# Four graph layers in one kernel: seams of layer 0, and group ends and maxima of layers 1 to 3

## Chip, cores and metric

One core of a Trainium2 chip runs the whole kernel in one launch. The metric is the time of one execution in device microseconds (us). TensorE (PE) does the matrix products, PEld is its weight load, VectorE (DVE), ScalarE (ACT) and GpSimd (POOL) do the rest; SyncE (SP) issues most DMAs, POOL some of them.

## What is computed

There are N = 2708 nodes with F = 512 features and one 0/1 adjacency matrix `adj` with about 1.2% ones and a full diagonal, all in float32. Four layers follow each other, and after each `x = layernorm(x + layer(x, adj))`. Cut to what matters:

```python
# layer 0: H = 4 heads of 128; _batchnorm over all nodes; att is the same for both uses
Xw  = einsum('hnd,hde->hne', Xh, W)
sig = sigmoid(f1[:, :, None] + f2[:, None, :])
att = masked_softmax(adj * sig, adj != 0)
Xn  = batchnorm(att @ Xw)                       # first pass over the attention
emb = batchnorm(elu(Xn @ Wm.T + bm) + Xn)       # encoder block
Y   = elu((att @ emb) @ W.T)                    # second pass
out = batchnorm(elu(Y @ Wd.T + bd) + Y)         # decoder block
# layer 1
x1 = (A @ (x @ W + b)) / deg[:, None]
# layer 2
e = (x @ edge_w) @ (x @ edge_w).T               # symmetric
x2 = adj * softmax(x @ node_w, 0) * softmax(where(adj > 0, e, NEG), 1) @ (x @ weight) + bias
# layer 3
x3 = softmax((x @ Wq + bq) @ (x @ Wk + bk).T / sqrt(F) + 2 * adj) @ (x @ Wv + bv)
```

## The kernel before

N is 21 blocks of 128 rows and a last one of 20 (REST; Q = 32). The code is written in the order of the work, and a planner fixes each engine's order when the program is built, from program order and its own estimate of when operands are ready; `tc.issue_after` puts instructions behind a given one on their engine. Engines then run strictly in that order.

**Layer 0** keeps everything transposed: attention weights are made tile by tile, 128 sources by half of the targets (1354) by two heads. `attention_pass` runs twice. In each, four rounds (half `hf`, head pair `p`) go over the 22 blocks in `ORDER`, the REST block in place 11. `form` makes a tile `t` (four buffers): tanh on ACT (L385, two operations), a masked product on DVE (L393, 2.97 us), Exp on ACT (L394). Then twelve matrix instructions add it to `po` (L460; each float32 `matmul` call is two of them). In the first pass, `p == 0` also prepares the mask `a` (L374, L375) and stores it to `adj_d`. Column sums come from a product with ones (`psm`, L483), in places 4 to 19 of `p == 1` for two tiles at once, added first on DVE (L477). Some tiles are stored to DRAM (`kept`, L442) and loaded in the second pass by SP (L445), where the other tiles load `a` from `adj_d` (L358) and `count` finds zeros (L335).

`keep` ends a round of the first pass: copies from PSUM, sums to DRAM and back as reciprocals (L583, L588, L589), and after the second round a `small_product` (vector times matrix and turned, L535, L538, L540) for the encoder's bias. After the pass, `batch_scale` gives scale1 and mean1; four products (L685) make `mqk = Wq Wk^T / sqrt(F)` for layer 3; the encoder's weights are scaled in place (L673, L677); the encoder (L713) follows with another `small_product` inside for mean1, with the second pass's first tiles formed beside it. `decode` ends a round of the second pass; its last call does the decoder's remaining products (L848) and `centre`. Then scale3 and shift3 (L521, L529), L972 on ACT, L979 on DVE, and transposes and products into `hid_hi`/`hid_lo` (L985, L117).

**Layer 1** takes four blocks of targets at a time: `raw` loads, L1037 turns them into 0/1, L1044 multiplies. Row normalizations are put off in `later`.

**Layers 2 and 3** share `softmax_layer`, with targets in 7 groups of three blocks (the last has four). `one_score` computes a tile of scores (L1203, or transposes of stored ones, L1195) and a running maximum (L1251); the REST block is split over four column sections and added up with `quarters` (L1227, L1236, L1237). `spread_max` at a group's end turns the maxima (L1263), reduces them (L1266), and spreads them over all partitions (L1269, L1274, L1287). `one_sum` subtracts, exponentiates, adds to `acc` (L1294, L1295, L1298, L1305), in layer 2 multiplies with `adj` (L1500), and multiplies with the values (L1310). It runs `lag = NT + 3` steps behind. `end` closes a group (L1360, L1370; layer 2: L1505, L1506; layer 3: L1356, then L1388, L1587).

Of the kernel before, what the change touches and what calls it, by code (L numbers as in the profile page):

```python
# [17 lines left out]
P = 128  # L18
# [11 lines left out]
def gnn_stack_kernel(  # L30
# [49 lines left out]

    def rows_tile(name):
        return big.tile([P, NT, F], F32, tag="rows", name=name)
# [71 lines left out]
    mqk_d = dram.tile([C, P, C, P], F32, name="mqk_d")  # L154
    qscale = float(1.0 / F**0.5)
# [4 lines left out]
    with ExitStack() as l0:  # L160
# [160 lines left out]
        def attention_pass(values, first, att, psum, finish, f1b=None, blocks=(), spread=None, rest=None, taken={}):  # L321
# [83 lines left out]
            for hf, (h0, w) in enumerate(HSPAN):  # L405
                for p in range(H // HP):
# [13 lines left out]
                    before = None  # L420
                    for place, jt in enumerate(ORDER):
# [8 lines left out]
                        if kept is None or first:  # L430
                            rows = n if n == P else HR
                            with ExitStack() as order:

                                for ins in taken.values() if place == 2 else ():
                                    order.enter_context(tc.issue_after(ins.ins))
                                step = form(hf, p, jt, att, prepare, f1b, t[:rows, :, :w])
                            if rest is not None:
                                rest(step)
                                rest = None
                                sums = sum_tiles()  # L440
                            if kept is not None:
                                nc.gpsimd.dma_start(kept[:n, :, :w], tv)  # L442
                        else:
                            for r in range(0, P if n == P else HB * Q, P if n == P else Q):
                                nc.sync.dma_start(t[r : r + n, :, :w], kept[:n, :, :w])  # L445
                            if p == 0 and jt in KEPT[1]:
                                count(hf, jt, att)
                        if po is None:


                            both = [
                                psum.tile([P, HP, BANK], F32, tag=f"po{q}", name="po", bufs=1)
                                for q in range(HB)
                            ]
                            po = [both[q][:, k, :] for k in range(HP) for q in range(HB)]
                        for k in range(HP):
                            h = HP * p + k
                            for q, (q0, qw) in enumerate(HCH[hf]):
                                r = 0 if n == P else q * Q
                                nc.tensor.matmul(  # L460
                                    po[HB * k + q][:, :qw],
                                    values[r : r + n, jt, h * P : (h + 1) * P],
                                    t[r : r + n, k, q0 : q0 + qw],
                                    start=(place == 0),
                                    stop=(place == NT - 1),
                                )
# [3 lines left out]
                        if prepare or not ALONE <= place < NT - LAST:  # L470
                            whole, m = t, n
                        elif place % 2 == 0:
                            before = t
                            continue
                        else:
                            whole, m = before, P
                            nc.vector.tensor_tensor(  # L477
                                whole[:n, :, :w], whole[:n, :, :w], tv, ALU.add
                            )
                        for k in range(HP):  # L480
                            for r, (q0, qw) in enumerate(SCH[hf]):

                                nc.tensor.matmul(  # L483
                                    sums[k][32 * r : 32 * r + 32, :SW],
                                    ones32[:m],
                                    whole[:m, k, q0 + qw - SW : q0 + qw],
                                    start=(place == 0),
                                    stop=(place == NT - 1),
                                )
# [62 lines left out]
        with (  # L552
# [8 lines left out]
            def keep(hf, p, po, sums):  # L561
# [10 lines left out]
                if hf == 0 and p == 1:  # L572
                    row = att.tile([P, HW], F32, tag="z", name="row", bufs=1)[:1, :F]
                    ps = small_product(po[0], mlp_w[0], prm_sb[:, B_ENC, :], row)
                    nc.vector.tensor_tensor(bias[:, 0, :], ps, prm_sb[:, MB_ENC, :], ALU.add)
# [55 lines left out]
            scale1, mean1 = batch_scale(stats, G_ENC, "bn1")  # L631

# [30 lines left out]
        with (  # L663
# [3 lines left out]

            (enc_w,) = mlp_w  # L670
            for c in range(C):
# [9 lines left out]
            mqk = emb[:, NT - 3 * C : NT - 2 * C, :]  # L681
            for c in range(C):
                ps = psum.tile([P, F], F32, tag="misc", name="ps_m", bufs=2)
                for o in range(C):
                    nc.tensor.matmul(  # L685
                        ps,
                        wqT[:, o, c * P : (c + 1) * P],
                        wkT[:, o, :],
                        start=(o == 0),
                        stop=(o == C - 1),  # L690
                    )
                nc.scalar.activation(mqk[:, c, :], ps, AF.Copy, scale=qscale)
            for o in range(C):
                nc.gpsimd.dma_start(mqk_d[o], mqk[:, :, o * P : (o + 1) * P])

            row = emb[:1, NT - 3 * C - 2 : NT - 3 * C, :]
# [8 lines left out]
            for ci, (c0, w) in enumerate(CHUNKS):  # L705
                pss = []
                for o in range(C):
# [13 lines left out]
                    if ci == 0 and o == 0:  # L721
                        pm = small_product(
                            psum.tile([P, F], F32, tag="misc", name="ps_mean", bufs=2),
                            enc_w,
                            mean1,
                            row[:, 1, :],
                        )
                        nc.vector.tensor_tensor(bias[:, 0, :], bias[:, 0, :], pm, ALU.subtract)
                        nc.vector.tensor_scalar(
                            bias[:, 1, :], bias[:, 0, :], 1.0, None, ALU.subtract  # L730
                        )
# [27 lines left out]
            spare = []  # L759

# [35 lines left out]
            def decode(hf, p, po, rb):  # L796
# [45 lines left out]
                def mlp(q, o, st, wide):  # L842
# [4 lines left out]
                    for c in range(C):  # L847
                        nc.tensor.matmul(  # L848
# [73 lines left out]
                for q in range(HB):  # L922
# [10 lines left out]
                    mlp(q, 3, st, True)  # L933

# [11 lines left out]
    with (  # L946
# [66 lines left out]
        for g in range(0, NT, G):  # L1013
# [12 lines left out]
            for jt, (j0, m) in enumerate(BLOCKS):  # L1026
# [5 lines left out]
                if m < P or w < len(group) * P:  # L1032
                    nc.vector.memset(raw[:, : len(group) * P], 0.0)
                for r in range(0, P if m == P else 2 * Q, P if m == P else Q):
                    nc.sync.dma_start(raw[r : r + m, :w], adjT[j0 : j0 + m, c0 : c0 + w])
                with tc.issue_after(ready[0].ins) if g == 0 and jt < 5 else nullcontext():
                    nc.vector.tensor_scalar(  # L1037
                        a[:, : len(group) * P], raw[:, : len(group) * P], 0.0, None, ALU.not_equal
                    )
                halves = (hid_hi, hid_lo) if m == P else (hid_hi,)  # L1040
                for it in group:
                    at = a[:, (it - g) * P : (it - g + 1) * P]
                    for k, half in enumerate(halves):
                        nc.tensor.matmul(  # L1044
                            pos[it],
# [12 lines left out]
        for y, n in later:  # L1058
            layer_norm(y, y, n)
# [13 lines left out]

    quarters = featp.tile([P, C, Q], F32, name="quarters")
    for c in range(C):
        nc.vector.tensor_tensor(
            quarters[:, c, :], ident[:, :Q], ident[:, Q : 2 * Q], ALU.add
        )
        for k in range(2, C):
            nc.vector.tensor_tensor(  # L1080
                quarters[:, c, :], quarters[:, c, :], ident[:, k * Q : (k + 1) * Q], ALU.add
            )
    quarters = quarters.rearrange("p c q -> p (c q)")
# [32 lines left out]
    def softmax_layer(  # L1116
# [12 lines left out]
        def key_order(gi):  # L1129

            late = list(range(NFULL // 2)) + [NT - 1] + list(range(NFULL // 2, NFULL))
            if not mirror:

                return late if gi else list(range(NT))
# [118 lines left out]
        def spread_max(st):  # L1253
# [3 lines left out]
            k = len(GROUPS[gi])  # L1257
            tp = psum.tile([P, C, P], F32, tag="tp", name="tp_mx")
            nm = small.tile([P, GB], F32, tag="nm", name="nm")
            dg = att.tile([P, GB, P], F32, tag="dg", name="dg", bufs=1)  # L1260
            for b, it in enumerate(GROUPS[gi]):
# [3 lines left out]
                )  # L1265
                nc.vector.tensor_reduce(  # L1266
                    nm[:n, b : b + 1], tp[:n, b, :], AX.X, ALU.max, negate=True
                )
                nc.vector.tensor_scalar(  # L1269
                    dg[:n, b, :n], ident[:n, :n], nm[:n, b : b + 1], None, ALU.mult  # L1270
                )
            pb = psum.tile([P, BANK], F32, tag="tp", name="pb")
            full = sum(BLOCKS[it][1] == P for it in GROUPS[gi])
# [15 lines left out]
        def one_sum(st, k):  # L1289
# [6 lines left out]
            if k == 0:  # L1296
                st["acc"] = att.tile([P, GW], F32, tag="acc", name="acc", bufs=1)
                nc.vector.tensor_copy(st["acc"][:, :w], e)  # L1298
                st["po"] = [
                    psum.tile([P, F], F32, tag=f"po{(GROUP * gi + b) % C}", name="po", bufs=1)  # L1300
                    for b in range(C if after is not None else len(GROUPS[gi]))
                ]
# [3 lines left out]
            if weigh:  # L1306
                weigh(e, load_a(gi, jt)[:, :w])

# [39 lines left out]
        def end(st):  # L1348
# [19 lines left out]
            for b, it in enumerate(GROUPS[gi]):  # L1368
# [15 lines left out]

                def project(b=b, it=it, n=n):
# [14 lines left out]

        def score_step(t):
# [4 lines left out]
            if k == NT - 1:  # L1406
                spread_max(states[gi])

        def sum_step(t):
            gi, k = divmod(t, NT)  # L1410
            if t == 0:
                last_values()
            one_sum(states[gi], k)
# [12 lines left out]
    with (  # L1426
# [3 lines left out]
        for gi, group in enumerate(GROUPS):  # L1430
            c0, w = GSPAN[gi]
# [273 lines left out]
```

## Time and profile before

| | |
|---|---|
| median of 3 runs | 3321.99 us (3317.25 to 3322.62) |
| profiled execution | 3319.34 us, span 3317.5 us |
| mean granted TensorE clock | 0.99 |
| layer 0, first pass / encoder / second pass with decoder | about 0 to 585 / 585 to 700 / 692 to 1197 us |
| layer 1 | about 1200 to 1511 us |
| layer 2 / layer 3 | about 1511 to 2316 / 2317 to 3317 us |
| DMA | 381 MB, mean 115 GB/s |

A profile's group is one line, engine, operation and tile: count, busy time, mean of one in ns, and after the second bar the idle time of the engine just before them with what ended it. A window gives for a stretch its length and each engine's busy time, then the granted clock (1 is full), the share of DMA time and GB/s. Times are from the span's start.

### The profile page before, as it was taken

Reading aid. Unit: us, or ns where it says so; the run is one execution under the profiler, and the core shown is the slowest. Engines: PE = TensorE matmul, PEld = TensorE weight load, DVE = VectorE, ACT = ScalarE, POOL = GpSimd, SP = SyncE. Lnnn points to the kernel's source line nnn. Section 1 sums busy time; section 2 is a strip of 40 time slices with the busy share of each in tenths; the row PEclk is TensorE's granted clock in tenths of the full one; section 3 lists DMA queues with packets and bytes.
Section 4 is the critical chain, followed back from the end, with each engine's and each line's share of the span. In section 5 each row is a group of like instructions: output and inputs, shape, how many; then the busy total and the mean of one; then the engine's idle time right before and its main releaser. Section 6 shows DMA issues by size and latency. Waiting matters only on the chain.

```text
span 3317.5 us, 30401 instructions
## 1 busy us (share of the span) xinstructions
PE 3232.7 (97%) x10920; PEld 1725.2 (52%) x10920; DVE 1971.7 (59%) x3221; ACT 1319.5 (40%) x1497; POOL 130.1 (4%) x211
## 2 busy tenths in 40 slices
PE   8998999999999999999999999999999999999999
PEld 5443444454444446885554555444455555555554
DVE  7877977767687685445135667776353443543533
ACT  6887887457868652001133333332021010110111
POOL 1100100000000000000010000000000000000000
PEclk9999999999999999999999999999999999999999
DMA  8855863335555412540044444553211111111100
GB/s 289 299 189 169 310 214 123 105 108 199 177 176 175 161 40 84 144 123 15 1 127 128 119 124 134 148 148 108 69 46 34 42 34 42 40 32 45 36 24 20
DMA packets 172550, 381.45 MB, mean 115 GB/s; under 512 B 20938, under 2 KB 115094, under 8 KB 167982
## 3 DMA queue, kind: packets, MB, share of 16 engines
q1 hardware_dynamic: 156926, 308.16, 30.7%
q0 software_dynamic: 15472, 71.33, 5.8%
q8 instruction: 86, 1.41, 0.2%
q14 instruction: 66, 0.54, 0.1%
HBM read 307.22 MB, written 71.67 MB: 114 GB/s over the span
## 4 chain that ended last, share of the span: by engine, by line
PE 76%; DVE 9%; issue 8%; DMA 4%; ACT 3%; POOL 0%; SPq 0%; DVEq 0%; POOLq 0%; ACTq 0%
PE po L1310 22%; PE ps_s L1203 17%; PE po L460 11%; PE ps_nb L1044 6%; PE ps_wide L1105 4%; DVE t L393 3%; PE ps_hid L117 2%; PE ps_sup L1447 2%; PE ps_o L1388 2%; PE ps_mlp L713 2%; PE ps_dec L848 2%; DMA a<-adj_d 1%; ACT t L394 1%; DMA a_cols<-in_adjT_dram 1%; PE psm L483 1%
## 5 line engine op out<-in xcount | busy, mean ns | idle before, releaser
L393 DVE SCALAR_TENSOR_TENSOR t<-t,a 128x2708 f32<-128x2708 f32 (+1 forms) x156 | 462.1, 2974 | 125.0 <-ACT t L385 121.1
L385 ACT ACTIVATE t<-f1b,f2h 128x1354 f32<-128x1354 f32 (+1 forms) x312 | 428.1, 1413 | 61.7 <-PE po L460 28.0
L460 PE MATMUL po<-t,xw 128*128 128x452 f32 (+3 forms) x1056 | 415.1, 557 | 15.7 <-ACT t L394 15.7
L394 ACT ACTIVATE t<-t 128x2708 f32<-128x2708 f32 (+1 forms) x156 | 382.5, 2454 | 110.5 <-DVE t L393 110.3
L1310 PE MATMUL po<-sup,e 128*128 128x512 f32 x882 | 412.4, 602 | 6.2 <-DVE e L1500 5.9
L460 PE MATMUL po<-t,emb 128*128 128x452 f32 (+3 forms) x1056 | 400.3, 547 | 12.4 <-ACT t L394 9.1
L1310 PE MATMUL po<-e,xs 128*128 128x384 f32 (+1 forms) x1176 | 407.5, 489 | 0.0
L1203 PE MATMUL ps_s<-sup,hT 128*128 128x384 f32 (+1 forms) x1176 | 406.9, 490 | 0.0
L1581 DVE SCALAR_TENSOR_TENSOR e<-a_cols,ps_s 128x384 f32<-128x384 f32 (+1 forms) x154 | 85.6, 556 | 428.9 <-PE ps_s L1203 405.9
L460 PEld LDWEIGHTS po<-t,xw 128*128 128x128 f32 (+1 forms) x1056 | 191.2, 192 | 228.4 <-issue 201.7
L1203 PEld LDWEIGHTS ps_s<-sup,hT 128*128 128x128 f32 x1176 | 221.9, 190 | 164.2 <-issue 14.1
L460 PEld LDWEIGHTS po<-t,emb 128*128 128x128 f32 (+1 forms) x1056 | 193.5, 190 | 212.1 <-issue 187.3
L1310 PEld LDWEIGHTS po<-e,xs 128*128 128x128 f32 x1176 | 221.6, 190 | 157.2 <-issue 6.0
L1310 PEld LDWEIGHTS po<-sup,e 128*128 128x128 f32 x882 | 162.1, 192 | 173.9 <-issue 142.8
L1203 PE MATMUL ps_s<-hT 128*128 128x384 f32 (+5 forms) x672 | 212.3, 461 | 2.4 <-DVE e L1497 1.7
L97 ACT ACTIVATE ln_rstd<-ln_rstd 128x1 f32<-128x1 f32 x88 | 17.2, 201 | 495.0 <-DVE ln_rstd L96 494.7
L1496 ACT ACTIVATE a_cols<-a_cols,neg_big 128x384 f32<-128x384 f32 (+1 forms) x154 | 94.7, 616 | 239.0 <-DMA a_cols<-in_adjT_dram 190.7
L1044 PE MATMUL ps_nb<-hid_hi,at 128*128 128x512 f32 x484 | 185.6, 390 | 1.1 <-DVE at L1037 1.1
L1044 PE MATMUL ps_nb<-hid_lo,at 128*128 128x512 f32 x462 | 179.9, 389 | 0.0
L1305 DVE TENSOR_TENSOR acc<-acc,e 128x384 f32<-128x384 f32 (+2 forms) x294 | 162.4, 552 | 11.7 <-ACT e L1295 2.0
L1203 PEld LDWEIGHTS ps_s<-hT 128*128 128x128 f32 x672 | 122.4, 190 | 88.3 <-issue 17.3
L1294 DVE TENSOR_TENSOR e<-e,nmax 128x384 f32<-128x384 f32 (+1 forms) x308 | 154.5, 551 | 21.8 <-ACT nmax L1287 21.8
(247 smaller groups left out, 3316.8 us busy)
## 6 DMA issues: line engine op xcount, KB each, us to landing
a<-adj_d SPq DMA_DIRECT2D x110, 677.0 KB
a_cols<-in_adjT_dram SPq DMA_DIRECT2D x378, 192.0 KB
a<-in_adjT_dram SPq DMA_DIRECT2D x42, 677.0 KB
adj_d<-a POOLq DMA_DIRECT2D x42, 677.0 KB, 6.0
raw<-in_adjT_dram SPq DMA_DIRECT2D x105, 256.0 KB
kept<-t POOLq DMA_DIRECT2D x16, 1354.0 KB, 6.9
t<-kept SPq DMA_DIRECT2D x16, 1354.0 KB
a_cols<-in_adjT_dram SPq DMA_DIRECT2D x63, 202.0 KB
```

The lines of the kernel that those rows point to most:

```text
L385: nc.scalar.activation(tv[:, k, :], f1b[:n, k, :w], AF.Tanh, bias=f2h[:n, jt, h : h + 1], scale=0.5,)
L393: step = nc.vector.scalar_tensor_tensor(tv, tv, GUARD, ab, ALU.add, ALU.mult)
L394: nc.scalar.activation(tv, tv, AF.Exp, scale=0.5)
L460: nc.tensor.matmul(po[HB * k + q][:, :qw], values[r : r + n, jt, h * P : (h + 1) * P], t[r : r + n, k, q0 : q0 + qw], start=(place == 0), ...
L1044: nc.tensor.matmul(pos[it], at, half[:, jt, :], start=(jt == 0 and k == 0), stop=(jt == NT - 1),)
L1105: nc.tensor.matmul(ps[:, :width], w(c, o), xt(c), start=(c == 0), stop=(c == C - 1),)
L1203: nc.tensor.matmul(ps[:, b * P : w], keys[:, c, j0 : j0 + P], st["q"][:, c, b * P :], start=(c == 0), stop=(c == C - 1),)
L1294: nc.vector.tensor_tensor(e, e, st["nmax"][:, :w], ALU.add)
L1305: nc.vector.tensor_tensor(acc, acc, e[:m], ALU.add)
L1310: nc.tensor.matmul(out, lhsT, rhs, start=(k == 0), stop=(k == NT - 1))
L1496: nc.scalar.activation(a, a, AF.Identity, bias=neg_big[: a.shape[0]], scale=1.0e30)
L1581: nc.vector.scalar_tensor_tensor(e, a, 2.0, ps, ALU.mult, ALU.add)
```

## The change

Layer 0:

- The small product after the second round of the first pass is gone. One small product with `shift1 = beta - mean1 * scale1` and the unscaled encoder weights, before they are scaled, gives the bias; the one inside the encoder is gone too.
- A pair's addition and its product with ones are issued after the next tile is formed, ahead of that tile's products.
- In the second pass kept tiles are loaded by GpSimd's queue in place of SP's.
- Only two of the four products for `mqk` stay before the encoder. Wk^T and half of Wq^T go to DRAM, come back after the decoder's last call, and the other two products are issued behind the decoder's last matmul.

Layers 1 to 3:

- Layer 1's last group works on its real width (148 columns in place of 256, 20 rows in place of 128), and its last two normalizations are issued in layer 2's second group. `quarters` is made at the start of the kernel.
- `spread_max` reduces and multiplies all full blocks of a group at once, and is issued after the first score of the next group.
- Subtraction, Exp, `acc` and the product with `adj` are split off as `one_exp`, issued one step ahead of the product with the values; `acc` has two buffers.
- In layer 3's first group the REST block is last but one. The kernel's last block is projected in four column sections at once (as `quarters` needs it), added up afterwards, and before two earlier blocks in part.

```diff
-                                nc.sync.dma_start(t[r : r + n, :, :w], kept[:n, :, :w])
+                                nc.gpsimd.dma_start(t[r : r + n, :, :w], kept[:n, :, :w])
...
+                        if waiting is not None:
+                            waiting()
+                            waiting = None
                         for k in range(HP):
...
+                        if single:
+                            add_up(t, n, None, place == 0, place == NT - 1)
                         else:
+                            waiting = partial(add_up, before, P, tv, False, False)
...
-                if hf == 0 and p == 1:
-                    row = att.tile([P, HW], F32, tag="z", name="row", bufs=1)[:1, :F]
-                    ps = small_product(po[0], mlp_w[0], prm_sb[:, B_ENC, :], row)
-                    nc.vector.tensor_tensor(bias[:, 0, :], ps, prm_sb[:, MB_ENC, :], ALU.add)
...
             scale1, mean1 = batch_scale(stats, G_ENC, "bn1")
+            shift1 = batch_shift(scale1, mean1, B_ENC, "bn1")
...
+            merged(0)
+            (enc_w,) = mlp_w
+            pm = small_product(..., enc_w, shift1, row[:, 1, :])
+            nc.vector.tensor_tensor(bias[:, 0, :], pm, prm_sb[:, MB_ENC, :], ALU.add)
...
+            nc.gpsimd.dma_start(wkT_d, wkT)
+            nc.gpsimd.dma_start(wqT_d, wqT[:, :, half * P :])
+            merged(1)
...
+                nc.sync.dma_start(wk_again, wkT_d)
+                nc.sync.dma_start(wq_again, wqT_d)
+                mqk = att.tile([P, HW], F32, tag="a", name="mqk_rest", bufs=3)[:, : half * F]
+                with tc.issue_after(last_dec[0].ins):
+                    for c in range(half):
+                        for o in range(C):
+                            nc.tensor.matmul(po[1 + c], wq_again[...], wk_again[:, o, :], ...)
+                for c in range(half):
+                    nc.scalar.activation(mqk[:, c, :], po[1 + c], AF.Copy, scale=qscale)
+                for o in range(C):
+                    nc.gpsimd.dma_start(
+                        mqk_d[o][:, half:, :], mqk[:, :, o * P : (o + 1) * P]
+                    )
...
-        for y, n in later:
-            layer_norm(y, y, n)
+        last_rows = later
...
-                return late if gi else list(range(NT))
+                return late if gi else list(range(NFULL - 1)) + [NT - 1, NFULL - 1]
...
+            for b, count, n in [(0, full, P)] + [
+                (b, 1, BLOCKS[GROUPS[gi][b]][1]) for b in range(full, k)
+            ]:
+                some = slice(b, b + count)
                 nc.vector.tensor_reduce(
+                    nm[:n, some], tp[:n, some, :], AX.X, ALU.max, negate=True
+                )
+                nc.vector.tensor_tensor(dg[:n, some, :n], ident..., nm..., ALU.mult)
...
-                st["acc"] = att.tile([P, GW], F32, tag="acc", name="acc", bufs=1)
+                st["acc"] = att.tile([P, GW], F32, tag="acc", name="acc", bufs=2)
...
+                    later[-2:] = [project_parts, before, project_sum, last]
...
+            if k == 0 and gi > 0:
+                spread_max(states[gi - 1])
+            if t == total - 1:
                 spread_max(states[gi])
...
+                one_exp(states[0], 0)
+            if t + 1 < total:
+                one_exp(states[(t + 1) // NT], (t + 1) % NT)
             one_sum(states[gi], k)
...
+            for y, n in last_rows if gi == 1 else ():
+                layer_norm(y, y, n)
```

## The prediction

> **What bounds the kernel now.** I read the page's first two parts, then the chain of waits.
>
> ```profile
> PE 3232.7 (97%) x10920; PEld 1725.2 (52%) x10920; DVE 1971.7 (59%) x3221; ACT 1319.5 (40%) x1497; POOL 130.1 (4%) x211
> ...
> PEclk9999999999999999999999999999999999999999
> ...
> PE 76%; DVE 9%; issue 8%; DMA 4%; ACT 3%; POOL 0%; SPq 0%; DVEq 0%; POOLq 0%; ACTq 0%
> ```
>
> TensorE is the bound nearly everywhere: 97% busy, 76% of the chain, and "issue" between its pieces. Time comes off in two ways only: fewer matmuls on PE, or less waiting of PE. I looked for the waits in the timeline and asked for a table of the stretches that hold the long ones (length, PE busy, ..., granted clock):
>
> ```profile
> core 0: us, PE busy (x) PEld busy (x) DVE busy (x) ACT busy (x) POOL busy (x), PEclk, DMA share, GB/s
> 234.00:242.00 8.00, 6.59 (x34) 2.61 (x29) 6.96 (x3) 7.59 (x6) 0.00 (x0) 0.79 0.44 123
> 272.00:280.00 8.00, 5.31 (x17) 2.52 (x10) 6.33 (x3) 8.00 (x6) 0.53 (x1) 0.79 0.56 173
> 298.00:317.00 19.00, 9.99 (x40) 4.10 (x40) 14.91 (x16) 9.27 (x7) 2.24 (x4) 0.73 0.45 136
> 508.00:516.00 8.00, 6.59 (x31) 2.74 (x26) 6.96 (x3) 7.58 (x5) 0.00 (x0) 0.79 0.42 121
> 546.00:553.00 7.00, 5.03 (x9) 2.58 (x10) 5.84 (x6) 7.00 (x5) 0.53 (x1) 0.76 0.24 81
> 798.00:806.00 8.00, 5.13 (x10) 2.58 (x11) 8.00 (x11) 2.46 (x1) 0.00 (x0) 0.79 0.83 292
> 908.00:915.00 7.00, 6.22 (x12) 2.85 (x13) 7.00 (x9) 6.65 (x5) 0.00 (x0) 0.76 0.70 206
> 1196.00:1212.00 16.00, 8.48 (x21) 4.00 (x20) 14.96 (x34) 12.54 (x22) 0.00 (x0) 0.68 0.50 157
> 2202.00:2212.00 10.00, 7.84 (x21) 3.05 (x19) 7.72 (x18) 2.86 (x5) 0.00 (x0) 0.66 0.49 144
> 2283.00:2294.00 11.00, 7.22 (x11) 3.17 (x12) 11.00 (x33) 3.04 (x5) 0.00 (x0) 0.69 0.28 75
> 2425.00:2437.00 12.00, 8.92 (x18) 4.66 (x19) 6.48 (x16) 3.15 (x6) 0.00 (x0) 0.72 0.13 33
> ```
>
> In these 114 us PE is busy 77.3, so it idles 36.7. The clock is low as well: length times (1 - clock), summed over the rows, is 30.5 us, part of it laid over the idle time. All of it together, 67 us, is the most that the waits can give. Eleven stalls, and the change touches the code at each one.
>
> **The change part by part.** Groups, a wait of SP's queue and the timeline at one seam give the prices:
>
> ```profile
> L685 PE MATMUL ps_m<-emb 128*128 128x512 f32 x32 | 14.0, 594 | 0.9 <-DVE ft L627 0.9
> L477 DVE TENSOR_TENSOR t<-t 128x2708 f32<-128x2708 f32 (+1 forms) x16 | 47.6, 2974 | 17.3 <-PE po L460 13.9 <-ACT t L385 2.0 <-ACT t L394 1.4
> L335 DVE TENSOR_SCALAR_CACHE_REDUCE z<-a 128x1354 uint8<-128x1354 f32 (+1 forms) x44 | 68.6, 1560 | 33.7 <-DMA a<-adj_d 33.5
> L442 POOL DMA_DIRECT2D kept<-t x20 | 11.0, 552 | 215.9 <-ACT t L394 215.9
> ```
> ```profile
> SPq L445 <- PE po L460: 45.3, 11, 10.6
> ```
> ```profile
> 303.51 1.05 PE L540 MATMUL po<-ones,row 1*128 1x1 f32 x8 [0.77 <-DVE row L538]
> 312.80 1.12 PE L460 MATMUL po<-t,xw 128*128 128x452 f32 x1 [8.24 <-ACT t L394]
> ```
>
> *Merged weights, taken out of the MLP seam.* 16 of the 32 matmuls of L685 leave a stretch in which PE is busy 19.6 of 20 us (585 to 605): 14.0 / 2 = 7.0 us. The small product with shift1 replaces the one with mean1 (8 matmuls of 592 ns at 0.43 us spacing, eight tiny ones): nothing. New: it waits for two DVE operations of 0.16 us (covered by merged(0), 3.4 us), and the scaling of enc_w (L673, two of 0.71 us on ACT; two on DVE) now waits for it; merged(1), 3.4 us, covers that. Without that cover it costs 1 to 2 us. POOL gets two stores (1.0 and 0.5 MB) ahead of mqk_d's; pass 2 needs POOL only after 690. Value -6.5, ends -8 and -3.
>
> *Merged weights at the end of pass 2.* The same 7.0 us go into 1196 to 1212, where PE idles 7.52 us in one piece before tp_out (L985). After it, ps_hid takes 858 ns a matmul in that window against 606 in its group: 9 x 0.25 = 2.3 us come back if PE does not cool. Two ACT copies (0.585 us each) can stand before L972's first operation, the one that everybody waits for. The two loads on SP need the f1b slots, free since 1127.5. L955's memset and L965 on DVE follow in queue; if their memory is that of a tile that the last four POOL stores (0.91 us each to issue, 4.1 to land) still read, DVE holds everything for 8 us. Value -2, ends -3 and +8.
>
> *The small product in pass 1's seam (298 to 317).* DVE comes to L374 at 304.68, behind L538 and L575; without them at 300.1. The tile waited for at 312.80 then comes up to 4.6 us earlier. But L589's reciprocal stands before L393 in DVE's order and needs a load that SP issued at 302.25. Value -3, ends -4.6 and 0.
>
> *Pair sums later, 16 of them.* Windows 234, 272, 508 and 546 idle 7.5 us and lose up to 6.7 us to the clock. The next tile's L393 is no longer behind an add of 2.97 us. But 13.9 of the 17.3 us that DVE idles before these adds it waits for PE to finish reading the tile, and that stays; PE's order (po, sums, next po) stays too. Waiting behind the add on DVE are the next L393 and ACT's Exp; waiting for it is psm, with po queued behind it on PE. Value -2, ends -12 and +8.
>
> *Kept tiles loaded by POOL.* SP waits 45.3 us for a t slot with `a` loads queued behind, and DVE waits 33.5 us for `a`. Not all of it is SP's fault: at 793.88 DVE waits for a load that SP issued the moment the slot was free. Windows 798 and 908 idle 3.7 us and lose 3.4 to the clock; the wait that ends at 800.87 is 5.8 us long in all. POOL is idle there after L189. Value -4, ends -9 and +6. The row that prices POOL's side is L442: 552 ns an issue, 853 at most, with DVE busy beside it; nothing is added for starving. The Trainium skill, "SBUF — State Buffer", section "SBUF: two separate sides", speaks against the change: DMAs issued from GpSimd stand still while VectorE runs an operation in a two-port mode, since their descriptors cannot be written. By that rule each of the 28 loads could come late by such an operation, and L506's 0.69 us would make it at most 19 us; the sum goes by the row.
>
> *Layer 1's last rows and quarters.* PE waits 1.3 (L1095) and 2.6 us (L1447) around 1511 to 1515, the second behind two layer norms and the quarters on DVE, and 1.1 us for L1037 at 1490 and 1495. The first stays. Narrower memsets and masks are hidden under PE. Value -3, ends -4.5 and -0.5.
>
> *Layer 2's group ends.* Windows 2202 and 2283 idle 5.9 us and lose up to 6.8 to the clock; from 1810 to 2305 PE is busy 484.4 of 495, so 4.7 more lie scattered. At 2282.85 PE has finished pr, and the next product starts at 2286.78: DVE must do L1370, L1505, L1506 (2.06 us), the acc copy and L1500 first. With a second acc and exp and weigh one step ahead, that product is ready, six of them last 2.6 us, and the next needs DVE until 2286.1: 0.6 us of 3.9 stay. So 3.3 plus 2.7 of clock here, 3 at 2202, 1 elsewhere. spread_max comes one step (some 5 us) later; its nmax stood ready 15 us before use at 1931. Value -10, ends -16 and -2.
>
> *Layer 3's first group (2425 to 2437).* PE idles 3.1 us while L1266 and L1269 alternate with L1263, and 3.4 us is clock. With the REST tile one earlier and 10.3 us of ps_wide before spread_max nothing of this is waited for. Value -6, ends -7 and -2.
>
> *Tail.* 8 matmuls (3.4 us) become eight 32-column ones (1.05 us, as L1339's groups) and two of 0.43: -1.5; the last block's store is 256 KB instead of 40: +0.5. Value -1, ends -2 and +1.
>
> Sum: 6.5 + 2 + 3 + 2 + 4 + 3 + 10 + 6 + 1 = 37.5 off the profiled execution, 3319.34 (span 3317.5 and 1.8 around it): 3281.8. The median of the runs shown, 3321.99, is 2.65 above it: 3284.5, so **3285**.
>
> On the clock the rows decide: 234 to 242 is granted 0.79 with 1.41 us idle. The Trainium skill, "TensorE: Matmul & The Clock Gate", section "What's actually happening", has the half clock come after an idle window of about 3.4 us; most of these stalls would then cost their idle time alone, and the sum would be some 8 us smaller.
>
> **The rivals.** (1) *The stalls move.* The order on each engine is fixed when the program is built, and every edit lays it anew; DVE is busy 11 of 11 us in window 2283 and 8 of 8 in 798, so what PE no longer waits for there it may wait for a step later. What needs no such luck stays: 6.5 at the MLP seam, 6 in layer 3, 1 at the tail, 2 of layer 1: 3306. Against it: DVE is 59% busy over all. (2) *The adds turn into PE waits, slower.* Place: pass 1, second pair of heads, both halves. If the add starts one L393 later, psm waits 2.97 us longer with po behind it: 16 x 2.97 = 47.5, against 35.5 won elsewhere: 3322 + 12 = 3334. It decides from 35.5 / 16 = 2.2 us a pair. For it: PE takes psm before the next po. Against it: DVE is busy 92.2 of 126 us there (172 to 298), so it has room. (3) *Every stall goes, and the clock with it*: the good ends of all but the adds, 54 us: 3268. Against it: several releasers stand behind each stall.
>
> **How the numbers follow.** Forecast (25 to 48 us off) 0.50; rival 1 (7 to 25 off) 0.25; rival 3 0.07; rival 2, with other losses past 6.6 us, 0.12; no change 0.06. About 0.2%, 6.6 us, is what a measurement of this kernel can tell. Faster 0.82, same 0.06, slower 0.12. The unknown ends, added as squares, are about 13 us below and 21 above; with rival 1 and a part of "no change" taken in: 3262 to 3318.
>
> **What would show it.** Right: L685 with 16 matmuls at 585 and 16 new ones between 1197 and 1205; tp_out's gap under 2 us; no half clock at 2202, 2283 and 2425; windows 172 to 298 and 447 to 573 no longer than 126 us. Wrong: psm waiting for L477 in most pairs; t<-kept landing after PE wants it; DVE waiting at L955; new PE gaps after spread_max.

## The result and the profile after

| | before | changed |
|---|---|---|
| median | 3321.31 us (4 runs, 3317.25 to 3322.62) | 3300.57 us (4 runs, 3299.82 to 3307.07) |
| profiled execution, its span | 3319.34 us, 3317.5 us | 3307.07 us, 3305.3 us |
| mean granted clock | 0.99 | 0.991 |

The ratio is 0.9941, 95% interval 0.9928 to 0.9955: 20.7 us faster by the medians, where 37 were forecast. The profiled execution of the changed kernel is the slowest of its four, so the two traces differ by 12.2 us only. Every account below is made between the traces, so the losses in it are some us higher than in a usual execution: the edit of experiment 1 below takes off 31.5 us by the spans of the traces, 23.9 by the medians.

The page of the changed kernel, first two parts and the chain:

```profile
PE 3219.8 (97%) x10906; PEld 1720.2 (52%) x10906; DVE 1944.7 (59%) x3144; ACT 1347.9 (41%) x1512; POOL 149.1 (5%) x245
...
PEclk9999999999999999999999999999999999999999
...
PE 61%; DVE 1%; DMA 0%; ACT 0%; issue 0%; SPq 0%; DVEq 0%; ACTq 0%
```

PE is still the bound, and nothing in these lines says that a part of the change went wrong. One group of the page hints at it: PE's idle time ahead of the second pass's products, before and changed.

```profile
L460 PE MATMUL po<-t,emb 128*128 128x452 f32 (+3 forms) x1056 | 400.3, 547 | 12.4 <-ACT t L394 9.1
```
```profile
L478 PE MATMUL po<-t,emb 128*128 128x452 f32 (+3 forms) x1056 | 407.4, 554 | 33.4 <-ACT t L409 30.9
```

Where the time went shows when the execution is cut at events that both kernels have (first and last `po` product of a round, first `tp_w`, `tp_emb`, `tp_out` and so on); the cuts are starts and ends of PE's matmuls in the two traces:

| stretch | before, us | changed, us | difference |
|---|---|---|---|
| start to the first `po` product | 43.3 | 45.6 | +2.3 |
| first pass, rounds 0 and 1 | 254.8 | 255.4 | +0.6 |
| seam between the two halves | 14.75 | 1.21 | -13.5 |
| first pass, rounds 2 and 3, to `tp_w` | 260.0 | 260.1 | +0.2 |
| encoder: `tp_w` to `tp_emb` | 50.0 | 43.5 | -6.5 |
| second pass: `tp_emb` to the last `po` product | 517.9 | 547.8 | **+29.9** |
| decoder's end and seam, to the first `ps_nb` | 152.3 | 158.9 | +6.6 |
| layer 1, to layer 2's first `tp` | 218.2 | 217.2 | -1.0 |
| layer 2's projections, to the first `ps_s` | 162.8 | 160.1 | -2.7 |
| layer 2, to layer 3's first product | 726.7 | 707.1 | **-19.7** |
| layer 3 | 916.8 | 908.3 | -8.5 |

The table of windows, at the places in the changed trace that answer to those of before, and at a new one (731):

```profile
core 0: us, PE busy (x) PEld busy (x) DVE busy (x) ACT busy (x) POOL busy (x), PEclk, DMA share, GB/s
237.00:245.00 8.00, 6.59 (x34) 2.69 (x29) 6.96 (x3) 7.58 (x6) 0.00 (x0) 0.79 0.46 126
275.00:283.00 8.00, 5.30 (x13) 2.41 (x10) 7.05 (x4) 8.00 (x6) 0.53 (x1) 0.79 0.57 187
296.00:305.00 9.00, 9.00 (x40) 4.05 (x36) 6.47 (x7) 8.04 (x7) 0.53 (x1) 1.00 0.51 162
500.00:508.00 8.00, 6.59 (x34) 2.61 (x28) 6.96 (x3) 7.58 (x5) 0.00 (x0) 1.00 0.39 117
537.00:544.00 7.00, 4.77 (x13) 2.49 (x14) 6.10 (x6) 7.00 (x4) 0.53 (x1) 1.00 0.26 75
731.00:739.00 8.00, 4.08 (x11) 1.82 (x6) 2.29 (x2) 3.77 (x2) 0.00 (x0) 0.79 0.69 260
790.00:798.00 8.00, 2.14 (x3) 1.18 (x4) 8.00 (x11) 4.53 (x3) 0.39 (x1) 0.72 0.72 264
908.00:917.00 9.00, 2.47 (x4) 1.25 (x5) 9.00 (x12) 7.58 (x5) 0.00 (x0) 0.78 0.29 89
1216.00:1232.00 16.00, 8.80 (x21) 3.88 (x20) 14.36 (x32) 15.90 (x27) 2.91 (x4) 0.68 0.48 169
2208.00:2218.00 10.00, 10.00 (x42) 4.98 (x40) 9.71 (x28) 5.19 (x7) 0.00 (x0) 1.00 0.59 168
2287.00:2298.00 11.00, 10.25 (x32) 3.31 (x30) 11.00 (x29) 4.30 (x7) 0.00 (x0) 1.00 0.30 74
2432.00:2444.00 12.00, 12.00 (x41) 7.17 (x40) 7.53 (x17) 4.79 (x8) 0.00 (x0) 1.00 0.19 51
```

The stalls of layers 2 and 3 (last three rows) and of the first pass's seam (296) are gone but for 0.75 us at 2287, with their half clock. The stalls of the pair sums (237, 275, 500, 537) stand as before, PE's busy time within 0.01 us in three of the four; the half clock came at two of them only. The second pass has a new stall (731), and its two stalls at the start of a round are longer: the waits at 790 and 908 are 6.5 and 6.8 us, before 5.8 and 3.2 (at 798 and 908). Over the whole pass PE idles 35.0 us, before 12.6; the other 7.5 of the 29.9 us are longer busy time. The seam after the decoder (1216) idles 7.2 us of 16.

Groups of instructions (the pair's addition, the count of zeros, the merged products, the kept loads) answer to the groups of before:

```profile
L497 DVE TENSOR_TENSOR t<-t 128x2708 f32<-128x2708 f32 (+1 forms) x16 | 47.6, 2975 | 13.7 <-PE po L478 10.9 <-ACT t L400 1.7 <-ACT t L409 1.2
L350 DVE TENSOR_SCALAR_CACHE_REDUCE z<-a 128x1354 uint8<-128x1354 f32 (+1 forms) x44 | 68.6, 1560 | 81.1 <-DMA a<-adj_d 81.0
...
L698 PE MATMUL ps_m<-emb 128*128 128x512 f32 x16 | 9.3, 723 | 0.9 <-DVE ft L651 0.9
L982 PE MATMUL po<-wk_again,wq_again 128*128 128x512 f32 x16 | 7.0, 592 | 0.0
...
L460 POOL DMA_DIRECT2D t<-kept x28 | 14.6, 524 | 513.8 <-PE po L478 289.5 <-issue 134.3 <-ACT t L400 45.6
```

DVE waits 81.0 us for `a` before the counts, 33.5 before the change. With one kind of load moved off SP's queue, DVE waits longer for the loads that stayed on it. The timeline of the second pass shows how; DVE first, then two answers of SP's queue:

```profile
728.50 1.57 DVE L350 TENSOR_SCALAR_CACHE_REDUCE z<-a 128x1354 uint8<-128x1354 f32 x1 [3.69 <-DMA a<-adj_d]
729.99 0.08 DVE L350 DVE_READ_ACCUMULATOR z<-a 128x1 f32 x1
729.99 2.97 DVE L408 SCALAR_TENSOR_TENSOR t<-t,a 128x2708 f32<-128x2708 f32 x1
738.67 1.57 DVE L350 TENSOR_SCALAR_CACHE_REDUCE z<-a 128x1354 uint8<-128x1354 f32 x1 [5.71 <-DMA a<-adj_d]
740.15 0.08 DVE L350 DVE_READ_ACCUMULATOR z<-a 128x1 f32 x1
740.15 2.98 DVE L408 SCALAR_TENSOR_TENSOR t<-t,a 128x2708 f32<-128x2708 f32 x1
747.20 1.57 DVE L350 TENSOR_SCALAR_CACHE_REDUCE z<-a 128x1354 uint8<-128x1354 f32 x1 [4.07 <-DMA a<-adj_d]
```
```profile
732.99 0.32 SPq L373 DMA_DIRECT2D a<-adj_d  x1
...
743.16 0.32 SPq L373 DMA_DIRECT2D a<-adj_d  x1
```

The masked product (L408) ends at 732.96, SP issues a load of `a` at 732.99, it reaches DVE at 738.67, and the count that waited for it starts, with the next masked product behind it; that one ends at 743.13, and so on. It is a ring: `a` has three buffers, and DVE's order, as built, puts the count of a tile two masked products ahead of its own. The count then needs a load into the very buffer that the product just done has freed. Counted in the built order: 24 of the 44 counts stand two products ahead in the changed kernel, 11 before.

### The profile page after: what moved, and what is told of

It is laid out like the page before. It is cut to its first block, busy times and chain, and to the rows that moved or that the text cites. A ratio compares the mean times of both kernels' runs of the same rounds, so it can differ in the third digit from the quotient of the medians.

```text
span 3305.3 us, 30376 instructions
## 1 busy us (share of the span) xinstructions
PE 3219.8 (97%) x10906; PEld 1720.2 (52%) x10906; DVE 1944.7 (59%) x3144; ACT 1347.9 (41%) x1512; POOL 149.1 (5%) x245
## 3 DMA queue, kind: packets, MB, share of 16 engines
q8 instruction: 86, 1.41, 0.2%
## 4 chain that ended last, share of the span: by engine, by line
PE 61%; DVE 1%; DMA 0%; ACT 0%; issue 0%; SPq 0%; DVEq 0%; ACTq 0%
PE po L1374 23%; PE ps_s L1253 17%; PE ps_nb L1106 6%; PE ps_wide L1155 4%; PE ps_hid L129 2%; PE ps_sup L1551 2%; PE ps_o L1482 2%; PE ps_s L1245 1%; PE tp L1145 1%; DMA a_cols<-in_adjT_dram 0%; PE ps_parts L1277 0%; PE pb L1331 0%; PE ps_s L1287 0%; PE tp_out L1046 0%; PE po L1403 0%; PE pr L1424 0%
## 5 line engine op out<-in xcount | busy, mean ns | idle before, releaser
L408 DVE SCALAR_TENSOR_TENSOR t<-t,a 128x2708 f32<-128x2708 f32 (+1 forms) x156 | 461.9, 2975 | 101.5 <-ACT t L400 97.8
L478 PE MATMUL po<-t,emb 128*128 128x452 f32 (+3 forms) x1056 | 407.4, 554 | 33.4 <-ACT t L409 30.9
L1352 ACT ACTIVATE e<-e 128x384 f32<-128x384 f32 (+1 forms) x308 | 151.7, 522 | 117.3 <-DVE e L1351 114.4
L109 ACT ACTIVATE ln_rstd<-ln_rstd 128x1 f32<-128x1 f32 (+1 forms) x88 | 17.2, 201 | 395.1 <-DVE ln_rstd L108 394.7
L1351 DVE TENSOR_TENSOR e<-e,nmax 128x384 f32<-128x384 f32 (+1 forms) x308 | 163.1, 552 | 23.3 <-ACT nmax L1344 23.3
```

The costliest lines, as they stand in the source:

```text
L408: step = nc.vector.scalar_tensor_tensor(tv, tv, GUARD, ab, ALU.add, ALU.mult)
L478: nc.tensor.matmul(po[HB * k + q][:, :qw], values[r : r + n, jt, h * P : (h + 1) * P], t[r : r + n, k, q0 : q0 + qw], start=(place == 0), ...
L1351: nc.vector.tensor_tensor(e, e, st["nmax"][:, :w], ALU.add)
L1352: nc.scalar.activation(e, e, AF.Exp)
```

## The experiments

**1. Kept tiles on SP again** (changed kernel).

```diff
-  nc.gpsimd.dma_start(t[r : r + n, :, :w], kept[:n, :, :w])
+  nc.sync.dma_start(t[r : r + n, :, :w], kept[:n, :, :w])
```

> The changed kernel with the second pass's kept tiles loaded by SP again, as before; all else as changed. The second pass, from the first tp_emb product to the last po product, took 518 us before and 547.8 after. If GpSimd's queue is the cause in any way, that stretch falls back to 518 to 521 and the time to about 3272 us. If another part of the change (later start, other order in layer 0) made the pass longer, it stays near 548 and the time near 3300.

Measured: 3276.72 us, ratio 0.9872 (0.9857 to 0.9887); the second pass takes 522.4 us, so 25.5 of the 29.9 us lost there hang on this line. The built order is that of before again, with 11 of 44.

**2. That line alone** (kernel before, `sync` to `gpsimd`).

> The kernel before with one edit: kept tiles of the second pass loaded by GpSimd's queue. If that edit alone costs what the pass lost, the second pass grows from 518 to 545 to 548 us and the time to about 3350 us (slower). By the prediction's term it would be 4 us faster, with 9 faster and 6 slower as its ends: 3312 to 3327.

Measured: 3343.94 us against 3320.08, ratio 1.0075 (1.006 to 1.009): 24 us slower, second pass 545.9. The built order has the same 24 of 44, and DVE waits for `a` before the counts as in the changed kernel:

```profile
L335 DVE TENSOR_SCALAR_CACHE_REDUCE z<-a 128x1354 uint8<-128x1354 f32 (+1 forms) x44 | 68.7, 1562 | 84.5 <-DMA a<-adj_d 84.4
```

**3. The order alone** (changed kernel, loads still on GpSimd's queue).

```diff
-  if not first and p == (jt in KEPT[0]):
-      count(hf, jt, att, a)
...
   step = nc.vector.scalar_tensor_tensor(tv, tv, GUARD, ab, ALU.add, ALU.mult)
+  if not first and p == (jt in KEPT[0]):
+      with tc.issue_after(step.ins):
+          count(hf, jt, att, a)
```

> The changed kernel, kept tiles still on GpSimd's queue, with one order changed: the count of zeros of a tile (L350) is put behind that tile's own masked product (L408) on DVE. Theory 1 (order): in the changed kernel 24 of the 44 counts stand two masked products ahead, so that a count needs a load into the slot that the product behind it must free first; with that gone the second pass falls from 548 to 520 or less and the time to about 3270. Theory 2 (transfers): the kept loads on a second queue share the DMA engines and make the mask loads land late; then this changes the pass by less than 5 us and the time stays at 3295 to 3301.

Measured: 3273.86 us, ratio 0.9862 (0.9847 to 0.9877), second pass 519.9. Its group of the counts, against the one above, and a stretch of DVE's timeline:

```profile
L350 DVE TENSOR_SCALAR_CACHE_REDUCE z<-a 128x1354 uint8<-128x1354 f32 (+1 forms) x44 | 68.5, 1557 | 0.1
```
```profile
709.97 2.97 DVE L406 SCALAR_TENSOR_TENSOR t<-t,a 128x2708 f32<-128x2708 f32 x1
712.87 1.56 DVE L350 TENSOR_SCALAR_CACHE_REDUCE z<-a 128x1354 uint8<-128x1354 f32 x1
```

Each count now follows its own tile's product, and DVE no longer waits for `a` (0.1 us), with the same transfers on the same queues. So the order was the cause, not the DMA engines.

**4. The memset off DVE** (changed kernel; `nc.vector.memset(hid_hi...)` to `nc.gpsimd.memset`).

> The changed kernel with the memset of hid_hi's last block (L1016) on GpSimd in place of DVE. Theory: on DVE it waits for GpSimd's stores of the late merged weights and holds the copy of w_sb behind it, for which ps_hid waits 5.5 us; without it ps_hid starts about 5 us earlier and the time falls by 4 to 6 us, to about 3295. Rival: ps_hid is held by the scaled output anyway (DVE L1040 behind ACT), and the time stays within 1 us of 3300.6.

Measured: 3300.73 us, no difference: a miss. PE's wait for `w_sb` is 5.0 us in place of 5.5. DVE's timelines, of the changed kernel and of this one, say why:

```profile
1223.85 0.48 DVE L1016 MEMSET hid_hi<- 128x512 f32 x1 [0.40 <-DMA mqk_d<-mqk_rest]
1224.25 1.16 DVE L1026 COPY w_sb<-xs 128x2048 f32<-128x2048 f32 x1
```
```profile
1221.07 1.23 DVE L1026 COPY w_sb<-xs 128x2048 f32<-128x2048 f32 x1 [0.27 <-DMA mqk_d<-mqk_rest]
```

Now the copy itself waits for the stores. Both tiles lie in pools opened after the attention pass has closed its own, so whichever comes first would wait for what still reads that memory; this is read from the code and these two waits.

**5. Two blocks without the copy** (experiment 3; `w1_held if it < 2 else w1_sb` in `ps_hid`'s product).

> The third experiment's kernel (3273.9 us) with ps_hid's products of the first two blocks reading w1_held in place of its copy w_sb. Theory: the copy of w_sb writes memory that the attention pass gave up, and so waits for GpSimd's last stores out of it, whichever engine does the memset; the two blocks' products (about 7 us) need no copy and fill the 5 us that PE waits: the time falls by 4 to 6 us, to about 3269. Rival: the loads of x that overwrite w1_held now come later and PE waits for them in place of w_sb: within 1.5 us of 3273.9.

Measured: 3280.34 us, `tp_out` to `ps_nb` 99.2 us in place of 93.5. By then the last loads of x had gone over `w1_held`, so the first two blocks were multiplied with x, and PE waited 3.4 us for those loads and 6.6 us for ACT behind them. It tells nothing of the theory.

**6. The same, with copy and loads behind the two blocks.**

```diff
-  nc.vector.tensor_copy(w1_sb, w1_held)          # and load_x(...) of the last chunks
...
+  if it == 2:
+      nc.vector.tensor_copy(w1_sb, w1_held)
+      for cj in range(len(early), NCH):
+          load_x(x_held, cj)
```

> The fifth experiment again, with its fault mended: there the last loads of x had already gone over w1_held when the first two blocks were multiplied with it. Here the copy of w_sb and those loads come after the two blocks' products. Theory: ps_hid starts without waiting for GpSimd's stores, the stretch from tp_out to ps_nb falls from 93.5 back to about 88, the time by 4 to 6 us to about 3269. Rival: PE waits as long at the third block, or for x: within 1.5 us of 3273.9.

Measured: 3269.02 us, ratio 0.9853 (0.9839 to 0.9866), the fastest version. `tp_out` to `ps_nb` takes 87.7 us. PE's timeline (`w1_held` lies in the memory that the profile calls `xs`):

```profile
1190.10 0.66 PE L1047 MATMUL tp_out<-ident,ot 128*128 128x128 f32 x4 [1.75 <-ACT mqk_rest L991]
1190.59 3.60 PE L129 MATMUL ps_hid<-xs,ot 128*128 128x512 f32 x8
1194.03 0.60 PE L1047 MATMUL tp_out<-ident,ot 128*128 128x128 f32 x4
1194.46 3.60 PE L129 MATMUL ps_hid<-xs,ot 128*128 128x512 f32 x8
```

The products start 0.5 us after `tp_out` (6.5 us in the changed kernel), and eight of them take 3.6 us; the clock granted from 1190.1 to 1198.1 is 1.00.

**7. The queues with the same order** (experiment 3, kept tiles on SP).

> The third experiment's kernel (3273.9 us) with the kept tiles on SP's queue. It compares the two queues with the same order of counts and masked products on DVE. Theory 1 (only the order mattered): the second pass stays within 3 us of 520 and the time at 3271 to 3277. Theory 2 (loads on GpSimd's queue take DMA time from the mask loads): SP is faster by more than 4 us, below 3270. The prediction's term (SP's queue blocked by waits for a slot): SP is slower by 4 us, about 3278.

Measured: 3273.39 us, ratio 0.986 (0.9846 to 0.9873): the two queues are worth the same once DVE's order is mended.

**8. All four merged products ahead of the encoder** (experiment 3, the part of the change that moves two of them undone).

> The third experiment's kernel (3273.9 us) with all four merged products ahead of the encoder, as before the change, none after the decoder. Theory: the 7 us that left the encoder were given back after the decoder (end of the second pass to ps_nb: 152.3 us before, 158.7 now), so the move is worth nothing: the encoder's stretch (tp_w to tp_emb) 7 us longer, the seam after the decoder 6 to 6.5 shorter, the time within 1.5 us of 3273.9. The prediction's terms (6.5 and 2 us gained) make it 8.5 us slower, 3282.

Measured: 3273.72 us against experiment 3's 3273.86. The encoder's stretch is 6.6 us longer, the stretch from the last `po` product to `ps_nb` 6.2 shorter. The move gave back at one seam what it took at the other.

**9. Pair sums as before** (experiment 3; `add_up(...)` called at once).

> The third experiment's kernel (3273.9 us) with the pair sums as before (added and multiplied right after the tile's own products). The prediction's term makes this 2 us slower (ends: 12 slower, 8 faster). From the traces, where rounds 1 and 3 of the first pass have the same stalls at the same places in both kernels, theory: no difference, within 1.5 us of 3273.9, the two rounds 125 and 122 to 126 us as in all runs so far.

Measured: 3275.58 us (3272.82 to 3277.68; experiment 3: 3272.39 to 3275.02), ratio 0.9869 (0.9854 to 0.9884). In the traces rounds 1 and 3 are 124.9 and 122.4 us in both. No effect that can be told: the medians differ by 1.7 us, inside the spread of the runs.

**10. The small product alone** (kernel before; the product after the first pass's second round and the one for mean1 replaced by one with shift1).

> The kernel before with one part of the change: the small product of the first pass and the one for mean1 replaced by one with shift1 behind the first merged product; all four merged products stay in their place, SP loads the kept tiles. Theory: the seam at 298 to 313 us loses all of its 13.5 us and the next round gives 3.5 back, so the time is 10 us lower, about 3310. By the prediction's term it is 3 us lower, 3317, with 3315.5 as its best end. Rival: the gain of the seam hangs on the later pair sums, and alone the product gives less than 5 us.

Measured: 3306.29 us against 3319.98, ratio 0.9962 (0.9949 to 0.9974): 13.7 us by the medians, 10.6 by the spans. The seam loses its 13.5 us without the later pair sums; the next round gives 4.4 back. By the medians the gain is more than the 10 us expected.

**11. `one_exp` not ahead** (experiment 3; called with `one_sum`, `acc` with one buffer).

> The third experiment's kernel (3273.9 us) with one_exp called for the same step as one_sum, not one ahead, and one acc buffer; spread_max as changed. It says how much of layer 2's 19.5 us (ps_s to ps_po: 726.7 before, 707.4) hangs on the step ahead. Theory: the stall after pr at a group's end (4.1 us of idle time before) and the half clock after it come back at one or two of the seven group ends: layer 2 at 713 to 719, the time 6 to 12 us higher, 3280 to 3286. Rival: the late spread_max alone removed the stalls: layer 2 within 2 us of 707.4.

Measured: 3288.64 us, ratio 0.9913 (0.99 to 0.9927): 14.8 us slower, nearly all in layer 2 (721.9 us, 14.6 longer), and more than the 6 to 12 us expected.

**12. `spread_max` at the group's end** (experiment 3).

> The third experiment's kernel (3273.9 us) with spread_max called at the group's end again, as before (its reduction and product still for all full blocks at once); one_exp ahead as changed. Theory: the stall in layer 3's first group (3.1 us idle and 3.4 of clock before) comes back at about half, since fewer DVE operations alternate with PE: 2 to 5 us, and in layer 2 another 3 to 6 us: the time 5 to 11 us higher, 3279 to 3285. Rival: batching alone was enough: within 2 us of 3273.9.

Measured: 3281.46 us, ratio 0.9893 (0.988 to 0.9907). Layer 2 does not change (707.1 us); layer 3 is 5.6 us longer. Layer 2 as a window in three traces (columns as above): the kernel before, the changed one, experiment 11.

```profile
1674.00:2400.70 726.70, 712.80 (x2230) 363.19 (x2230) 449.95 (x997) 239.78 (x461) 44.51 (x77) 0.99 0.44 126
```
```profile
1689.90:2397.00 707.10, 703.43 (x2231) 361.87 (x2232) 443.06 (x969) 256.21 (x475) 44.77 (x77) 1.00 0.46 130
```
```profile
1656.10:2378.00 721.90, 710.40 (x2230) 363.82 (x2230) 444.59 (x969) 239.37 (x461) 44.74 (x77) 0.99 0.44 127
```

Layer 3's first 100 us, in experiment 3 and in experiment 12, where PE idles 3.3 us again:

```profile
2364.60:2464.60 100.00, 100.00 (x332) 57.72 (x332) 53.43 (x119) 18.86 (x39) 2.23 (x4) 1.00 0.18 46
```
```profile
2364.90:2464.90 100.00, 96.74 (x320) 55.50 (x320) 52.95 (x117) 18.17 (x39) 2.23 (x4) 1.00 0.16 44
```

Of layer 2's 19.6 us, 10.2 are idle time (726.70 - 712.80 = 13.9 before, 3.7 after) and 9.4 are PE's busy time for the same matmuls. At most 6.8 of these are the clock: the record of before has two stretches of 6.83 us at half clock in this layer, at 2203 and 2285, and that of the changed kernel has none. In `tp_mx` alone PE is busy 2.4 us less (5.9 before, 3.5 after): its three or four transposes now follow each other and overlap.

## Why the prediction was right and where it was wrong

The sign, and the place of the time inside the range, were right. The forecast of 25 to 48 us off was not met: 20.7 lies in the band of rival 1 (7 to 25 off). That the time came as near as 16 us to 3285 is in part luck, since large misses of both signs cancel.

- *Merged weights out of the encoder*: -6.5 forecast, -6.5 in the stretch, 6.6 by experiment 8. Right. Experiment 8 is the better evidence: in the traces without these products in the encoder the stretch is anything from 40.9 to 43.5 us.
- *Merged weights after the decoder*: -2 forecast, +6.6 measured, experiment 8: 6.2. The danger was named with its price (+8, the stores' memory, DVE held) and then not taken as the value. `tp_out`'s gap fell to 1.75 us, as forecast, and the wait came one product later, at `ps_hid` (5.45 us), where the value of -2 had none; DVE waiting at the memset was one of the prediction's signs of being wrong. Experiments 4 and 6 show that the wait goes with the copy and not with the memset, and that 5 us come back when the first products do without it.
- *Small product at the seam*: -3 forecast (best -4.6), -13.5 at the seam and +3.7 in the next round. The step priced DVE's queue at the seam. The trace shows another wait: the product's row lay in the single buffer of `z`, so that no mask of the next round could be made before it was done. The first mask of that round on DVE, before and changed:

```profile
304.68 0.87 DVE L374 TENSOR_SCALAR z<-a 128x1354 f32<-128x1354 f32 x1
```
```profile
282.10 0.91 DVE L389 TENSOR_SCALAR z<-a 128x1354 f32<-128x1354 f32 x1
```

Before, it starts right behind the product; in the changed kernel, 19 us ahead of the seam. That the buffer is the reason is read from code and trace; a row in other memory wasn't tried.
- *Pair sums later*: -2 forecast, nothing that can be told (experiment 9: 1.7 us by the medians, inside the spread, and rounds of equal length in the traces). The bounds held. Rival 2, the adds as PE waits, did not come: rounds 1 and 3 take 125.6 and 122.4 us.
- *Kept tiles by GpSimd*: -4 forecast, with +6 as the worst, +29.9 measured. This is the step that failed. It asked what a queue blocks and what an issue costs; L460 issues in 524 ns (the prediction's row said 552), and its loads of 1354 KB land in 7.0 us (median). The prediction had seen the wait itself (at 793.88, a load issued the moment the slot was free), but took it for a limit of the gain and not for something that could grow. What it left out is that the same line also changes the order that the planner lays for DVE: 24 counts stand two products ahead in place of 11. How the planner comes to that order was not looked into. Experiments 1 to 3 and 7 settle the rest: the line alone costs 24 us, and one order put right takes all of that back with the line in place. A fourth buffer for `a`, which would also open the ring, was not tried.
- *The rule that spoke against it*. The Trainium skill, "SBUF — State Buffer", section "SBUF: two separate sides", has transfers issued from GpSimd starve beside some VectorE operations. A slowdown came with the very transfers, and the rule would have been a ready story for it. Experiment 3 rules it out as the cause here: the same 28 loads on the same queue, the same operations on DVE, and no loss. Whether any operation of the second pass is of the kind that the rule speaks of, no run here shows.
- *Layer 1's end*: -3 forecast, -3.6.
- *Layer 2's group ends*: -10 forecast (best -16), -19.7. Mechanism right, size off: 7.3 us of idle time and 2.7 of clock were forecast, 10.2 of idle time and 9.4 of busy time came, at most 6.8 of the latter by the clock. Experiment 11 puts 14.6 on the step ahead, experiment 12 none on the late `spread_max`; the 5 that remain (the batched maxima among them) were not tried alone.
- *Layer 3's first group and tail*: -7 forecast, -8.5; 5.6 of it hang on the late `spread_max` (experiment 12).
- *Rivals*. Rival 1 said why (each edit lays the static order anew) and about how much (3306 against 3300.6), but not where, so its number is luck. It had layer 2 give nothing, which gave 19.7 us, and it had moved stalls cost only what they had given, while the second pass, which stood to gain 4 us, lost 29.9. Nor were the other terms right in sum: without the kept tiles' 4 us they make 33.5 off, and with the loads on SP (experiment 1) it was 43.4, mostly because the seam and layer 2 gave far more than forecast.

The 2.3 us at the start were not in the sum. Kernels with the same start come to their first `po` product at 43.1 to 45.6 us, so nothing is made of them.

## What to carry to other kernels

Where a planner lays each engine's order, moving a transfer to another queue also moves the instructions that wait for it: compare the built orders, and look for an instruction that waits for a load into a buffer which an instruction behind it must free. Cut two traces at common events before reading any group; the page's first line showed PE at 97% in both. Work moved into a gap is free only if what comes after the gap does not also wait for the moved work's stores; here it cost the 6 us that it had saved.

## What the runs showed of the hardware

The clock is not a function of the stall. The windows 237 to 245 and 500 to 508 of the changed kernel lie at the same place of rounds 1 and 3, each with 34 matmuls and 6.59 us of 8 busy; one was granted 0.79, the other 1.00. In the clock record of all traces here a stretch at half clock lasts 3.41 us or two to four times that (a trace's last one aside), and within a trace all of them start whole multiples of 3.413 us apart (before: 237.33, 274.88, 305.60), so each trace has a fixed grid. The stall at 237 and 500, a wait of 1.41 us for a pair's sum, stands 28 times in the 14 traces. The half clock follows it within 2.4 us in the 12 cases where it begins 1.10 to 2.08 us behind a point of that grid, and in none of the 16 others (0.08 to 1.09 us, and one at 3.39): the phase decides. The Trainium skill, "TensorE: Matmul & The Clock Gate", section "What's actually happening", has a free-running window of 3413 ns behind it; the grid agrees. Its idle window of about 3.4 us is no lower bound on the stall: 1.41 us of idle time were enough at 237. All stretches at half clock together cost at most 34.1 us before, 29.8 in the changed kernel and 19.5 in the fastest version (half their length, idle time included), so this part of a stall's price should be taken as a share of cases, not as a sum.
